# Inverse root on GpSimd, division in another slot, and spreads in column tiles: one change to a conditioned transformer block

## The chip, the cores and the metric

One core of one Trainium2 chip runs the whole kernel. The metric is the device time in microseconds (us) of one execution. TensorE multiplies matrices, VectorE and ScalarE work elementwise, GpSimd here issues DMAs that add as they write, and SyncE issues all other DMAs in its loop. The profile calls them PE, DVE, ACT, POOL and SP.

## The reference

The input x has 4 batches of 1024 tokens with 512 features; cond has 128 features for each batch. All is float32. Cut to what matters:

```python
def rmsnorm(x, t, gw, gb, bw, bb):              # t: the batch's condition
    g = (t @ gw.T + gb)[:, None, :]
    b = (t @ bw.T + bb)[:, None, :]
    return g * x * rsqrt(mean(x * x, axis=-1, keepdims=True) + 1e-6) + b

def attention(x):                                # 16 heads of 32 features
    q, k, v = heads(x @ Wq.T), heads(x @ Wk.T), heads(x @ Wv.T)
    p = softmax(einsum("blhd,bmhd->bhlm", q, k) / sqrt(32), axis=-1)
    return einsum("bhlm,bmhd->blhd", p, v).reshape(B, L, D) @ Wo.T

def swiglu(x):                                   # 2048 hidden features
    return silu(x @ gate_w.T) * (x @ hid_w.T) @ out_w.T

y = x + attention(rmsnorm(x, cond, first))
y = y + swiglu(rmsnorm(y, cond, second))
out = x + y
```

## The kernel before

**Layout.** Features lie on the 128 partitions and tokens along the free axis, in 8 blocks of 512 tokens (`NBLK`). Four heads of 32 features make a head group, and 256 queries (`HQ`) a half block. A step of the attention is one half block of queries of one head group against 256 keys. Four steps (`UN`) cover the 1024 keys, and 256 steps (`NR`) are all of the attention.

**The main loop** (line 768) runs over slots g, and each slot holds pieces of several steps: the scores of step g, the addition of the shift and the exponential of step g-5 (`r_x`), and the product with v of step g-6 (`r_v`). `kind = g % 4` is the slot's place in its round. A block has 32 slots (`BS`). The order on TensorE, VectorE, ScalarE and GpSimd is exactly the order in which the loop calls them (`manual_schedule`, line 698); what SyncE issues follows the order of the program, with a scheduler's freedom.

**Softmax.** The scores of four heads against 256 keys fill one PSUM tile (`sc`, line 310), and ScalarE copies them to `raw` (line 317). VectorE keeps an elementwise maximum in `rmax` (lines 322 and 325). In a slot of kind 0 TensorE transposes `rmax` (`mt`, line 331, full 128x128 array), VectorE reduces it to a maximum per query (line 337) and cuts minus that maximum into three bfloat16 parts, so that their sum keeps float32's accuracy (lines 339 to 342, tile `split`: 12 columns, three for each of 4 heads). In the next slot, kind 1, `parts_T` transposes the parts (`pt`, line 347), ScalarE copies the 12 rows to `mT` (line 349), and `spread` sends each head's maximum to all 128 partitions by a product with a 12x128 matrix of zeros and ones, `select` (`sp`, line 357), two heads at a time; ScalarE copies it to `shift` (line 358). `shifted` adds it to `raw` on VectorE (line 363), the exponential runs on ScalarE (line 366), and `weighted` multiplies with v (`av`, line 376).

**Row sums and division.** GpSimd's DMAs add the exponentials of steps 1, 2 and 3 of a round onto those of step 0 (line 390). In a slot of kind 0, VectorE folds the two halves (line 398), TensorE sums over partitions (line 408), ScalarE copies the sums to `total` (line 413). `inverse` takes their reciprocal (line 416, 128x256) and `normalize` multiplies with the product `avs` (line 425). Both stand at the end of that same slot of kind 0 (lines 900 to 904), ahead of the shift additions of the next slot, kind 1. For the one half block `GB`, `normalize` comes later.

**Tiling of TensorE.** `mm` (line 103) writes a product as one full-width matmul, or, if `columns[0]` is 32, as four matmuls on strips of 32 columns. Projections and feed-forward products are made of such strips in most slots; `sc` uses strips of 32 rows; `mt`, `pt` and `sp` use all columns.

**Feed-forward part.** From slot `FS` = 60 on, the slots also carry the gated feed-forward part of the block before: per two slots one chunk of 128 hidden features, with seven products in place of eight (`pair_15` to `pair_7`, tiles `pa` and `pb`) and one contraction into the output (`pc`, 32 matmuls, line 572), then the 24 chunks that are left run after the loop. Before slot 60 the slots carry the projections for keys, queries and values (`pkq`, `pv`) and the sums of weights (lines 474 to 477).

**The second norm** (lines 650 to 670; e is 32(n+1), less 4 for n > 0). For blocks n = 0 to 6: squares on ScalarE (line 132), their mean over features by a product with a constant matrix (`norm_mean`, line 145), copied to SBUF by ScalarE (line 151). All rows being alike, `compact` writes one row to DRAM (line 156), and `take` reads it back as 128x4 (`few`, line 162). At the end of slot e+20, `root` takes the square root on ScalarE (line 167), at e+20 or e+21 `invert` the reciprocal on VectorE (line 171); `put` writes the result to DRAM (line 176), and `norm_spread` reads it to all partitions (line 182). Scaling (line 193), modulation (line 196) and sums of tokens (lines 491 to 497) follow in slots g0+22 to g0+28. The norms of the first kind for later batches use a square root on ScalarE and a full reciprocal on VectorE (lines 143 and 632) in slots before 60.

What ends a slot of kind 0:

```python
            if kind == 0 and n_on and j_n < direct:
                inverse(j_n)

                if j_n != GB:
                    normalize(j_n)
            columns[0] = DH
            for fn, a in ended.pop(g, []):
                fn(*a)
```

Of the kernel before, what the change touches and what calls it, by code (L numbers as in the profile page):

```python
# [9 lines left out]

F32 = mybir.dt.float32
BF16 = mybir.dt.bfloat16
AF = mybir.ActivationFunctionType
ALU = mybir.AluOpType
# [3 lines left out]
P = 128  # L18
# [6 lines left out]
def tile_cond_transformer_block(  # L25
# [13 lines left out]
    nc = tc.nc  # L39
    NBLK, _, C, _ = x.shape  # L40
# [6 lines left out]
    DH = D // N_HEADS  # L47
    HG = P // DH
    FG = 4
    HQ = 256  # L50
# [6 lines left out]
    const = ctx.enter_context(tc.tile_pool(name="const", bufs=1))  # L57
    sb = ctx.enter_context(tc.tile_pool(name="sb", bufs=1))
# [5 lines left out]

    ident = const.tile([P, P], F32, tag="ident", name="ident")
    make_identity(nc, ident)
    ident_bf = const.tile([P, P], BF16, tag="ident_bf", name="ident_bf")
    make_identity(nc, ident_bf)
    ones_mean = const.tile([P, P], F32, tag="ones_mean", name="ones_mean")
    nc.vector.memset(ones_mean, 1.0 / D)  # L70
    ones_sum = const.tile([P, DH], F32, tag="ones_sum", name="ones_sum")
    nc.vector.memset(ones_sum, 1.0)
    eps = const.tile([P, 1], F32, tag="eps", name="eps")
    nc.vector.memset(eps, EPS)

    NP = 3 * HG
    split = [const.tile([P, QT, P], BF16, tag=f"split{i}", name=f"split{i}") for i in range(2)]
    for t in split:
        nc.vector.memset(t, 0.0)

    pick = const.tile([NP, HG], F32, tag="pick", name="pick")
    nc.vector.tensor_reduce(pick, ident[:NP, :NP].rearrange("p (h i) -> p h i", i=3), AX.X, ALU.add)
    select = const.tile([NP, HG, P], BF16, tag="select", name="select")
    nc.vector.tensor_copy(select, pick.unsqueeze(2).to_broadcast([NP, HG, P]))
    mod = const.tile([P, 4 * C, B], F32, tag="mod", name="mod")

    condT = const.tile([P, B], F32, tag="condT", name="condT")
# [15 lines left out]
    def mm(dst, w, moving, start: bool, stop: bool, seeded: bool = False):  # L103
        n = columns[0]
        for k in range(0, P, n):
            nc.tensor.matmul(  # L106
                dst[k : k + n, :], w[:, k : k + n], moving, start=start, stop=stop, skip_group_check=seeded
            )

    y, wkq, wv, wo, kq, v = {}, {}, {}, {}, {}, {}  # L110
    raw, rmax, shift, mT, av, acc, avs, oT = {}, {}, {}, {}, {}, {}, {}, {}
    x2, res, h, fw, ow = {}, {}, {}, {}, {}
    bank_a, bank_b, fifth = {}, {}, {}
    state = {}
# [13 lines left out]
    def norm_squares(dst, tag: str, k: int):  # L128

        sq = [sb.tile([P, NB], F32, tag="t", name=f"sq{tag}_{2 * k + i}", bufs=2) for i in range(2)]  # L130
        for i in range(2):
            nc.scalar.activation(sq[i], dst[:, 2 * k + i, :], AF.Square)
        if k == 0:
            state[tag] = sb.tile([P, NB], F32, tag="tot", name=f"tot{tag}", bufs=1)
            nc.vector.tensor_tensor(state[tag], sq[0], sq[1], ALU.add)
        else:
            for t in sq:
                nc.vector.tensor_tensor(state[tag], state[tag], t, ALU.add)
# [6 lines left out]
    def norm_mean(tag: str, inside: bool):  # L145
        if inside:
            pm = ps_av.tile([P, NB], F32, tag="av", name=f"pm{tag}")
        else:
            pm = ps.tile([P, NB], F32, tag="w", name=f"pm{tag}")
        mm(pm, ones_mean, state[tag], True, True)  # L150
        nc.scalar.copy(state[tag], pm)

    def compact(tag: str, t, rows: int, n: int):

# [3 lines left out]
    def take(tag: str):  # L158

        src = inv_s.pop(tag)  # L160
        few = sb.tile([P, src.shape[0] * src.shape[1] // P], F32, tag="few", name=f"few{tag}", bufs=2)
        nc.sync.dma_start(out=few, in_=src.rearrange("h (p c) -> (h p) c", c=few.shape[1]))
        state["few", tag] = few

    def root(tag: str):
        few = state["few", tag]
        nc.scalar.activation(few, few, AF.Sqrt, bias=eps)

    def invert(tag: str):
        few = state["few", tag]  # L170
        nc.vector.reciprocal(few, few)

    def put(tag: str):
        few = state.pop(("few", tag))
# [17 lines left out]
    def norm_scale(dst, tag: str, c: int):  # L192
        nc.vector.tensor_tensor(dst[:, c, :], dst[:, c, :], state[tag], ALU.mult)

    def norm_mod(which: int, b: int, dst, c: int):
        nc.scalar.activation(  # L196
            dst[:, c, :],
            dst[:, c, :],
            AF.Identity,
            bias=mod[:, (2 * which + 1) * C + c, b : b + 1],  # L200
            scale=mod[:, 2 * which * C + c, b : b + 1],
        )
# [141 lines left out]
    def parts_T(j: int):  # L344
        pt = ps.tile([P, HQ // P, P], BF16, tag="w", name=f"pt{j}")
        for qt in range(HQ // P):
            nc.tensor.transpose(pt[:, qt, :], split[j % 2][:, qt, :], ident_bf)
        mT[j] = sb.tile([NP, HQ], BF16, tag="mT", name=f"mT{j}", bufs=2)
        nc.scalar.copy(mT[j], pt[:NP, :, :].rearrange("p a b -> p (a b)"))

    def spread(j: int, k: int):

        if k == 0:
            shift[j] = sb.tile([P, HG, HQ], F32, tag="shift", name=f"shift{j}")
        pp = ps.tile([P, 2, HQ], F32, tag="w", name=f"sp{j}_{k}")
        for i in range(2):
            nc.tensor.matmul(pp[:, i, :], select[:, k + i, :], mT[j], start=True, stop=True)
        nc.scalar.copy(shift[j][:, k : k + 2, :], pp)  # L358

    def shifted(r: int, heads: slice = slice(0, HG)):  # L360
# [54 lines left out]
    def inverse(j: int):  # L415
        nc.vector.reciprocal(state["total", j], state["total", j])

    def normalize(j: int):

        m, qh = divmod(j, NB // HQ)  # L420
        n, hg = divmod(m, C)
        total = state.pop(("total", j))
        if (n, hg) not in oT:
            oT[n, hg] = sb.tile([P, NB], F32, tag=f"oT{hg}", name=f"oT{m}")
        nc.vector.tensor_tensor(oT[n, hg][:, qh * HQ : (qh + 1) * HQ], avs.pop(j), total, ALU.mult)
# [157 lines left out]
    GB = C * (NB // HQ)  # L583
    BS = GB * UN
# [9 lines left out]
    def pin(g, fn, *a):  # L594
        pinned.setdefault(g, []).append((fn, a))

    def between(g, fn, *a):
        halfway.setdefault(g, []).append((fn, a))

    def after(g, fn, *a):  # L600
        ended.setdefault(g, []).append((fn, a))
# [21 lines left out]
    for b in range(1, B):  # L623
        for half in range(QB):
            s = math.ceil((len(queue) + 1) / PACE)
            s4 = s - 4 - (s - 6) % UN
            tag = f"a{b}_{half}"
# [10 lines left out]
    FS = BS + 28  # L638
# [3 lines left out]
    for n in range(NBLK):  # L642
        g0 = (n + 1) * BS
        pin(g0 + 6, load_res, n)
        e = g0 if n == 0 else g0 - 4
        go = e + 13 if n < NBLK - 1 else g0 + 8
        for d in range(C):
            first.append((go, None, project_out, (n, d)))
            pin(go - 3 + (d // 2 * 4 if n else 0), load_wo, n, d)
        if n < NBLK - 1:  # L650
            tag = f"f{n}"
            after(e + 16, add_res, n)
            for k in range(2):
                after(e + 15 + k, lambda n=n, tag=tag, k=k: norm_squares(x2[n], tag, k))
            if n == 0:
                between(e + 17, norm_mean, tag, False)
            else:
                amid.setdefault(e + 17, []).append((norm_mean, (tag, True)))
            after(e + 17, norm_compact, tag)
            after(e + 19, take, tag)  # L660
            after(e + 20, root, tag)
            after(e + (20 if n == 0 else 21), invert, tag)
            after(e + (21 if n == 0 else 22), put, tag)
            after(e + (22 if n == 0 else 24), norm_spread, tag)
            scales, mods = ((24, 24, 25, 25), (25, 25, 26, 26)) if n == 0 else ((22, 22, 24, 24), (23, 23, 25, 25))
            for c in range(C):
                after(g0 + scales[c], lambda n=n, tag=tag, c=c: norm_scale(x2[n], tag, c))
                between(g0 + mods[c], lambda n=n, c=c: norm_mod(1, n // QB, x2[n], c))
            for i in range(4):
                after(g0 + (26, 26, 27, 28)[i] - (n > 0 and i == 0), token_sums, n, i)  # L670
# [27 lines left out]
    with tc.manual_schedule(  # L698
# [35 lines left out]
        direct = NR // UN - 2  # L734
        late = None
        g = 0
# [31 lines left out]
        while g < END:  # L768
            kind = g % UN
# [6 lines left out]
            j_n = g // UN - 3  # L776
            n_on = 0 <= j_n < NR // UN
            ffn = g >= FS
            p = (g - FS) // 2
# [3 lines left out]
            if kind == 1 and m_on:  # L783
                parts_T(j_m)
# [77 lines left out]
            else:  # L862
# [34 lines left out]
                    chain(g)()  # L897
                for fn, a in halfway.pop(g, []):
                    fn(*a)
            if kind == 0 and n_on and j_n < direct:  # L900
                inverse(j_n)

                if j_n != GB:
                    normalize(j_n)
            columns[0] = DH
            for fn, a in ended.pop(g, []):
                fn(*a)
# [4 lines left out]
        n = NBLK - 1  # L912
# [6 lines left out]
        for p in range(p0, NP_):  # L919
# [25 lines left out]
            if p == p0:  # L945
                pm = ps.tile([P, NB], F32, tag="w", name=f"pmf{n}")
# [54 lines left out]
```

## Time and profile before

| | |
|---|---|
| median of 3 runs | 2452.37 us (2448.12 to 2452.83) |
| the profiled execution | 2447.08 us, its span 2445.3 us, granted TensorE clock 0.997 |
| ScalarE's table loads, 1283 ns each | 13 before the exponential (L366), 7 at L167, 5 at L143, 4 elsewhere |
| VectorE's reciprocal of `total` (L416) | 64 of 1744 ns |
| VectorE's product with `avs` (L425) | 64 of 425 ns |
| spreads (L357), 12x128 weights, bfloat16 | 256 matmuls, 270 ns each |
| transposes of the parts (L347) | 128 matmuls, 219 ns each |
| ScalarE's square root of 128x4 (L167), VectorE's reciprocal of it (L171) | 7 of 298 ns, 7 of 169 ns |

A line of the timeline gives the start in us, the length, the engine, the line of the kernel, the operation, the written and the read tile, and how many instructions follow each other; in brackets the idle time ahead of it, and what ended it. Matmuls overlap, so a matmul's length is its latency, and the distance between the starts of two groups is what the first one takes of TensorE's time. A line of the waits gives who waited for whom, the total in us, how often, and the longest.

### The profile page before, as it was taken

The numbers are of one execution on the slowest core, as the hardware profiler recorded it, in microseconds if no ns is written. First come the engines' busy times: TensorE is split into PE (matmuls) and PEld (weight loads), VectorE is DVE, ScalarE is ACT, GpSimd is POOL, SyncE is SP. The second block draws the span as 40 slices with busy tenths as digits, with TensorE's granted clock in tenths as the row PEclk, the third lists the DMA queues.
The fourth block names the chain that finished last, engine by engine and source line by source line (L and its number), as shares of the span: only waits on it lengthen the run. The fifth ranks groups of instructions, "written<-read, shape, count | busy, mean of one in ns | idle before, by whom it ended". The sixth has DMA issues, their size and how long they took to land. (4 is left out here: it accounts for less than half of the span.)

```text
span 2445.3 us, 71149 instructions
## 1 busy us (share of the span) xinstructions
PE 2386.7 (98%) x31785; PEld 1128.7 (46%) x31785; DVE 1938.9 (79%) x2180; ACT 1416.2 (58%) x1495; POOL 172.8 (7%) x207
## 2 busy tenths in 40 slices
PE   8999999999999999999999999999999999999999
PEld 3333333334445544545454544454455445444544
DVE  2688888878889988999799979997999889843332
ACT  3677777666566655666566656665666566512110
POOL 0000000000000000000000000000000000000000
PEclk9999999999999999999999999999999999999999
DMA  6599999988888988889788988888888888853442
GB/s 214 168 284 253 250 256 235 232 205 216 206 201 208 220 224 197 208 215 234 195 208 208 237 206 197 209 226 211 206 205 206 226 200 205 212 165 118 143 129 71
DMA packets 185983, 501.70 MB, mean 205 GB/s; under 512 B 21319, under 2 KB 78663, under 8 KB 158286
## 3 DMA queue, kind: packets, MB, share of 16 engines
q0 software_dynamic: 28656, 208.68, 44.2%
q1 hardware_dynamic: 156734, 288.47, 35.5%
q8 instruction: 250, 4.10, 0.7%
q14 instruction: 55, 0.45, 0.1%
q10 hardware_dynamic: 288, 0.01, 0.0%
HBM read 246.44 MB, written 41.97 MB: 118 GB/s over the span
## 5 line engine op out<-in xcount | busy, mean ns | idle before, releaser
L317 ACT COPY raw<-sc 128x2048 f32<-128x2048 f32 x256 | 479.4, 1873 | 200.1 <-PE sc L310 133.4
L363 DVE TENSOR_TENSOR raw<-raw,shift 128x2048 f32<-128x2048 f32 (+1 forms) x320 | 589.0, 1856 | 3.3 <-ACT shift L358 2.8
L366 ACT ACTIVATE raw<-raw 128x2048 f32<-128x2048 f32 x256 | 490.2, 1915 | 128.9 <-DVE raw L363 124.8
L322 DVE TENSOR_TENSOR rmax<-rmax,raw 128x1024 f32<-128x1024 f32 x384 | 469.5, 1223 | 54.4 <-ACT raw L317 47.9
L106 PE MATMUL pc<-h,ow 128*32 128x512 f32 x4096 | 467.7, 593 | 3.3 <-DMA ow<-in_out_w 2.3
L376 PE MATMUL av<-raw,v 128*32 128x256 f32 x4096 | 275.8, 387 | 34.5 <-ACT raw L366 30.6
L390 POOL DMA_DIRECT2D raw<-raw x192 | 165.7, 863 | 1959.3 <-ACT raw L366 886.0
L310 PE MATMUL sc<-q,k 32*128 32x256 f32 x4096 | 293.3, 400 | 0.3 <-ACT raw L317 0.3
L106 PE MATMUL pa<-x,fa 128*32 128x256 f32 x4096 | 268.2, 379 | 0.3 <-DVE pa L524 0.2
L106 PE MATMUL pa<-sums,fw 128*32 128x256 f32 x4096 | 267.9, 379 | 0.0
L106 PEld LDWEIGHTS pc<-h,ow 128*32 128x32 f32 x4096 | 128.2, 110 | 246.7 <-issue 225.4
L310 PEld LDWEIGHTS sc<-q,k 32*128 32x128 f32 x4096 | 184.9, 184 | 116.6 <-issue 66.6
L106 PE MATMUL pkq<-y,wkq 128*32 128x512 f32 (+1 forms) x1664 | 234.3, 601 | 4.2 <-ACT y L196 4.1
L376 PEld LDWEIGHTS av<-raw,v 128*32 128x32 f32 x4096 | 107.4, 109 | 159.0 <-ACT raw L366 52.2
L106 PEld LDWEIGHTS pa<-x,fa 128*32 128x32 f32 x4096 | 131.1, 110 | 103.0 <-issue 8.8
L106 PEld LDWEIGHTS pa<-sums,fw 128*32 128x32 f32 x4096 | 133.1, 110 | 87.9
L577 DVE SCALAR_TENSOR_TENSOR res<-pc,res 128x512 f32<-128x512 f32 x128 | 88.2, 689 | 76.0 <-PE pc L106 75.0
L556 ACT ACTIVATE t<-pa 128x512 f32<-128x512 f32 x128 | 77.5, 605 | 109.9 <-PE pa L106 109.5
L539 ACT COPY pb<-pa 128x256 f32<-128x256 f32 x128 | 45.9, 359 | 160.3 <-PE pa L106 158.9
L106 PE MATMUL pb<-x,fw 128*32 128x256 f32 x2048 | 134.0, 379 | 1.2 <-ACT pb L539 1.2
L106 PE MATMUL pa<-x,fw 128*32 128x256 f32 x2048 | 135.2, 381 | 0.0
L106 PEld LDWEIGHTS pkq<-y,wkq 128*32 128x32 f32 (+1 forms) x1664 | 73.2, 118 | 131.5 <-issue 118.3
(106 smaller groups left out, 2214.4 us busy)
## 6 DMA issues: line engine op xcount, KB each, us to landing
raw<-raw POOLq DMA_DIRECT2D x192, 1024.0 KB, 9.1
fw<-sw SPq DMA_DIRECT2D x128, 512.0 KB, 7.5
fa<-in_gh_w SPq DMA_DIRECT2D x128, 384.0 KB, 6.5
ow<-in_out_w SPq DMA_DIRECT2D x128, 256.0 KB, 3.7
wkq<-in_kq_w SPq DMA_DIRECT2D x32, 512.0 KB, 5.9
v<-vs SPq DMA_DIRECT2D x128, 128.0 KB, 5.5
k<-kqs SPq DMA_DIRECT2D x124, 128.0 KB, 6.8
kqs<-st SPq DMA_DIRECT2D x61, 256.0 KB, 7.4
```

The source lines that it names most:

```text
L106: nc.tensor.matmul(dst[k : k + n, :], w[:, k : k + n], moving, start=start, stop=stop, skip_group_check=seeded)
L310: nc.tensor.matmul(sc[:, i, k, :], keys[rows, k * P : (k + 1) * P], queries[rows, :], start=True, stop=True)
L317: nc.scalar.copy(raw[r].rearrange("p k h q -> p h k q"), state.pop(("sc", r)))
L322: nc.vector.tensor_tensor(rmax[j], rmax[j], raw[r][:, k, :, :], ALU.max)
L363: nc.vector.tensor_tensor(t, t, s.unsqueeze(1).to_broadcast(list(t.shape)), ALU.add)
L366: nc.scalar.activation(raw[r], raw[r], AF.Exp)
L376: nc.tensor.matmul(av[j][i * DH : (i + 1) * DH, :], v[m, u][:, k, i * DH : (i + 1) * DH], raw[r][:, k, i, :], start=(kt == 0), stop=(kt == ...
L390: nc.gpsimd.dma_start(out=acc[j].rearrange("p k h q -> p (k h q)"), in_=raw[r].rearrange("p k h q -> p (k h q)"), accum_op=ALU.add,)
L539: nc.scalar.copy(bank_b[p][:, RIGHT], bank_a[p][:, RIGHT])
L556: nc.scalar.activation(state["t", p], bank_a[p], AF.Tanh, scale=0.5)
L577: nc.vector.scalar_tensor_tensor(r, pp, 0.5, r, ALU.mult, ALU.add)
```

## The change

It has four parts.

1. *Inverse root.* `norm_mean` now adds epsilon as it copies (Identity with a bias, for Copy). `root` and `invert` are replaced by `inverse_root`, all at the end of slot e+20: one VectorE instruction shifts the number's bits right by one and inverts them against a constant, which gives a first estimate of the inverse root up to a factor; GpSimd multiplies by that factor and takes four Newton steps of four instructions, 17 instructions on 128x4, each waiting for the one before. `put` stays where it was and reads GpSimd's result. In the built program these 17 stand in the Pool queue between the accumulate DMAs of slots e+20 and e+21, and SyncE's `put` keeps its place, between the `ow` load and the spread.
2. *Division.* `inverse` and `normalize` move from the end of a slot of kind 0 to the end of the slot two later (kind 2, the third), for all slots of kind 0 before 60 but that of the last half block of a token block, and from 60 on for those at places 12, 24 and 28 of a block. All others stay.
3. *Spreads.* `select` and `mT` get 128 rows, zero below the 12, and `spread` goes through `mm`: eight matmuls on strips of 32 columns for two on all columns. `mT` is two fixed tiles.
4. *Transposes of the parts* take 32 columns of `split` for 128.

```diff
--- before.py
+++ after.py
@@ -9,6 +9,7 @@
 from concourse._compat import with_exitstack
 
 F32 = mybir.dt.float32
+I32 = mybir.dt.int32
 BF16 = mybir.dt.bfloat16
 AF = mybir.ActivationFunctionType
 ALU = mybir.AluOpType
@@ -80,8 +81,14 @@
 
     pick = const.tile([NP, HG], F32, tag="pick", name="pick")
     nc.vector.tensor_reduce(pick, ident[:NP, :NP].rearrange("p (h i) -> p h i", i=3), AX.X, ALU.add)
-    select = const.tile([NP, HG, P], BF16, tag="select", name="select")
-    nc.vector.tensor_copy(select, pick.unsqueeze(2).to_broadcast([NP, HG, P]))
+
+
+    select = const.tile([P, HG, P], BF16, tag="select", name="select")
+    nc.vector.memset(select, 0.0)
+    nc.vector.tensor_copy(select[:NP], pick.unsqueeze(2).to_broadcast([NP, HG, P]))
+    parts_of = [const.tile([P, HQ], BF16, tag=f"mT{i}", name=f"mT{i}") for i in range(2)]
+    for t in parts_of:
+        nc.vector.memset(t, 0.0)
     mod = const.tile([P, 4 * C, B], F32, tag="mod", name="mod")
 
     condT = const.tile([P, B], F32, tag="condT", name="condT")
@@ -148,7 +155,7 @@
         else:
             pm = ps.tile([P, NB], F32, tag="w", name=f"pm{tag}")
         mm(pm, ones_mean, state[tag], True, True)
-        nc.scalar.copy(state[tag], pm)
+        nc.scalar.activation(state[tag], pm, AF.Identity, bias=eps)
 
     def compact(tag: str, t, rows: int, n: int):
 
@@ -158,17 +165,24 @@
     def take(tag: str):
 
         src = inv_s.pop(tag)
-        few = sb.tile([P, src.shape[0] * src.shape[1] // P], F32, tag="few", name=f"few{tag}", bufs=2)
+        few = sb.tile([P, src.shape[0] * src.shape[1] // P], F32, tag="few", name=f"few{tag}")
         nc.sync.dma_start(out=few, in_=src.rearrange("h (p c) -> (h p) c", c=few.shape[1]))
         state["few", tag] = few
 
-    def root(tag: str):
+    def inverse_root(tag: str):
+
         few = state["few", tag]
-        nc.scalar.activation(few, few, AF.Sqrt, bias=eps)
-
-    def invert(tag: str):
-        few = state["few", tag]
-        nc.vector.reciprocal(few, few)
+        y, t = (sb.tile(list(few.shape), F32, tag=f"few{i}", name=f"few{i}{tag}") for i in range(2))
+        nc.vector.tensor_scalar(
+            y.bitcast(I32), few.bitcast(I32), 1, 0x3FFFFFFF, ALU.logical_shift_right, ALU.bitwise_xor
+        )
+        nc.gpsimd.tensor_scalar_mul(y, y, 1.35 * 2.0**62)
+        for _ in range(4):
+            nc.gpsimd.tensor_tensor(t, y, y, ALU.mult)
+            nc.gpsimd.tensor_tensor(t, t, few, ALU.mult)
+            nc.gpsimd.tensor_scalar(t, t, -0.5, 1.5, ALU.mult, ALU.add)
+            nc.gpsimd.tensor_tensor(y, y, t, ALU.mult)
+        state["few", tag] = y
 
     def put(tag: str):
         few = state.pop(("few", tag))
@@ -344,9 +358,9 @@
     def parts_T(j: int):
         pt = ps.tile([P, HQ // P, P], BF16, tag="w", name=f"pt{j}")
         for qt in range(HQ // P):
-            nc.tensor.transpose(pt[:, qt, :], split[j % 2][:, qt, :], ident_bf)
-        mT[j] = sb.tile([NP, HQ], BF16, tag="mT", name=f"mT{j}", bufs=2)
-        nc.scalar.copy(mT[j], pt[:NP, :, :].rearrange("p a b -> p (a b)"))
+            nc.tensor.transpose(pt[:DH, qt, :], split[j % 2][:, qt, :DH], ident_bf)
+        mT[j] = parts_of[j % 2]
+        nc.scalar.copy(mT[j][:NP], pt[:NP, :, :].rearrange("p a b -> p (a b)"))
 
     def spread(j: int, k: int):
 
@@ -354,7 +368,7 @@
             shift[j] = sb.tile([P, HG, HQ], F32, tag="shift", name=f"shift{j}")
         pp = ps.tile([P, 2, HQ], F32, tag="w", name=f"sp{j}_{k}")
         for i in range(2):
-            nc.tensor.matmul(pp[:, i, :], select[:, k + i, :], mT[j], start=True, stop=True)
+            mm(pp[:, i, :], select[:, k + i, :], mT[j], True, True)
         nc.scalar.copy(shift[j][:, k : k + 2, :], pp)
 
     def shifted(r: int, heads: slice = slice(0, HG)):
@@ -658,8 +672,7 @@
                 amid.setdefault(e + 17, []).append((norm_mean, (tag, True)))
             after(e + 17, norm_compact, tag)
             after(e + 19, take, tag)
-            after(e + 20, root, tag)
-            after(e + (20 if n == 0 else 21), invert, tag)
+            after(e + 20, inverse_root, tag)
             after(e + (21 if n == 0 else 22), put, tag)
             after(e + (22 if n == 0 else 24), norm_spread, tag)
             scales, mods = ((24, 24, 25, 25), (25, 25, 26, 26)) if n == 0 else ((22, 22, 24, 24), (23, 23, 25, 25))
@@ -897,11 +910,16 @@
                     chain(g)()
                 for fn, a in halfway.pop(g, []):
                     fn(*a)
-            if kind == 0 and n_on and j_n < direct:
-                inverse(j_n)
-
-                if j_n != GB:
-                    normalize(j_n)
+            if n_on and j_n < direct and kind in (0, 2):
+
+
+                at = g - kind
+                in_first = j_n % GB == GB - 1 or (at >= FS and at % BS not in (12, 24, 28))
+                if in_first == (kind == 0):
+                    inverse(j_n)
+
+                    if j_n != GB:
+                        normalize(j_n)
             columns[0] = DH
             for fn, a in ended.pop(g, []):
                 fn(*a)
```

## The prediction

> **What bounds the kernel now.** I read the page first, then the waits of TensorE, then the timeline engine by engine. In what follows a slot is one pass of the main loop, a round is four slots (kind 0 to 3), about 31 us once the feed-forward part runs beside the attention, and a block is 32 slots, 256 us.
>
> ```profile
> span 2445.3 us, 71149 instructions
> PE 2386.7 (98%) x31785; PEld 1128.7 (46%) x31785; DVE 1938.9 (79%) x2180; ACT 1416.2 (58%) x1495; POOL 172.8 (7%) x207
> ...
> DVE  2688888878889988999799979997999889843332
> ```
>
> TensorE is the bound: 98% busy, and the same groups of matmuls follow at the same pitch over the whole run. What can be won is therefore (a) pitch, where the tiling of the array changes, and (b) the few places where TensorE waits. VectorE is at 8 to 9 tenths in the same slices, so it is the next bound.
>
> ```profile
> PE av L376 <- ACT raw L366: 30.6, 24, 3.5
> ...
> PE av L376 <- ACT totf L151: 3.3, 6, 0.6
> PE sum L408 <- PE pa L106: 2.8, 7, 0.7
> ```
>
> Nearly all waiting is `av` waiting for the exponential, 24 times. The next view is TensorE's timeline, first a slot with spreads (`sp`), then one without:
>
> ```profile
> 1197.41 1.05 PE L106 MATMUL pb<-x,fw 128*32 128x256 f32 x16
> 1198.40 0.27 PE L347 MATMUL pt<-ident_bf,split 128*128 128x128 bf16 x2
> 1198.60 1.15 PE L310 MATMUL sc<-q,k 32*128 32x256 f32 x16
> 1199.57 0.38 PE L357 MATMUL sp<-mT,select 12*128 12x256 bf16 x2
> 1199.88 1.07 PE L376 MATMUL av<-raw,v 128*32 128x256 f32 x16
> 1200.88 0.39 PE L357 MATMUL sp<-mT,select 12*128 12x256 bf16 x2
> 1201.20 1.07 PE L106 MATMUL pa<-x,fw 128*32 128x256 f32 x16
> ...
> 1213.60 1.05 PE L106 MATMUL pb<-x,fw 128*32 128x256 f32 x16
> 1214.57 1.15 PE L310 MATMUL sc<-q,k 32*128 32x256 f32 x16
> 1215.65 1.07 PE L376 MATMUL av<-raw,v 128*32 128x256 f32 x16
> ```
>
> Differences of starts are the true pitch: pb to sc 0.97, sc to av 1.08, av to pa 0.89, and pa to pa, with no change of tiling, 0.86. Last, three engines at two of the waits:
>
> ```profile
> 1235.37 1.28 ACT L366 ACT_TABLE_LOAD   x1
> 1236.66 1.91 ACT L366 ACTIVATE raw<-raw 128x2048 f32<-128x2048 f32 x1
> 1238.62 1.07 PE L376 MATMUL av<-raw,v 128*32 128x256 f32 x16 [1.27 <-ACT raw L366]
> ...
> 1307.69 2.29 DVE L363 TENSOR_TENSOR raw<-raw,shift 128x2048 f32<-128x2048 f32 x1
> ...
> 1315.62 0.64 PE L408 MATMUL sum<-raw,ones_sum 128*32 128x256 f32 x8 [0.36 <-PE pa L106]
> ```
>
> In the first three a table load delays the exponential and av stands 1.27. In the last two VectorE runs without a gap from 1301.6 to 1317.6, and the sum waits for the fold (L398) at its end.
>
> **What the Trainium skill says.** "TensorEngine Tiling (Array Packing)", Key Properties: a change of tiling mode drains TensorE. The trace agrees: 0.97 against 0.86 after pb. "ScalarE activation tables: per-element evaluation and per-set limits" puts two sets one load of 1283 ns apart; the trace has just that. "SBUF — State Buffer", Who interferes with whom: a VectorE instruction with two SBUF inputs and a GpSimd instruction that reads SBUF block each other fully. No run here shows it yet: GpSimd issues only DMAs after the start. "GPSIMD Engine Reference", section 3.1, prices long elementwise work alone, not 4 elements.
>
> **The change, part by part.** Signs: minus is time saved.
>
> *Spreads and part transposes on 32-column tiles.* The shown slot takes 0.99+0.20+0.97+0.31+1.00+0.32 = 3.79 from pb to pa. Then: pb to pt without a change of tiling 0.86 (-0.13); pt to sc, two transposes in one strip plus the 0.11 of a change, 0.22 to 0.29, I take 0.26 (+0.06); sc to sp like sc to av (+0.11); the first spread, now eight matmuls, unknown: at best two groups of four at the 0.10 that a full-width one now takes (0.20), at worst the fp32 rate of 0.054 each (0.43), I take 0.24 (-0.07); av to sp 0.89 (-0.11). Sum up to the second spread -0.14, bounds -0.22 and +0.08. Behind it ScalarE leads: shift copy, raw copy, avs copy and exponential follow without a gap, and end 0.12 before av is due in an ordinary round (1268.23 against 1268.35); a waiting av follows by 0.06. So of the 0.08 won on the second spread only 0.03 to 0.06 counts (-0.03; at worst +0.15, as a slower spread delays that chain). -0.17 over 50 rounds with feed-forward is -8.5 (-14 to +11). In the 13 early rounds the chain before pt is full-width, so that a change of tiling is added: zero.
>
> *Root and reciprocal to VectorE bits and GpSimd.* Seven square roots with their table loads go; the load that delays the exponential costs TensorE 1.28 each time (waits of 1.27 six times, 1.29 at 493.47), ScalarE being free at 1235.37: 7 x 1.28 = -9.0. Added are one VectorE instruction of about 0.18 (row L339), in a slot where the shift addition ends about 0.3 before ScalarE is free, and 17 GpSimd instructions in series. None of that kind is in the trace: at least 0.10 each (the memset at the start), at most the length of the VectorE instruction that each waits for, 1.22 to 2.28. I take 0.3, so 5 us, done near 1238, before `put` is issued now (1240.96). Behind them in the Pool queue stands one accumulate DMA (now 1231.78, landing in 9.1, its fold at 1252.6): 11 us spare. VectorE held up in turn: +1 over all (0 to +3). The copy with the epsilon bias is 0.10 longer (0.69 of L143 against 0.59); the exponential ahead of it comes 0.9 earlier: zero. Zeroing of the new tiles lies in VectorE's idle start.
>
> *Division to the third slot, before the feed-forward part.* There reciprocal and product (1.74 and 0.42, 2.1 from start to start) stand before the shift addition of the second slot. The waits of av there are 3.46, 1.99, 0.26, 2.00, 3.46, 1.48 and 1.13 (at 160, 227, 260, 294, 361, 427, 461); each falls by at most 2.1: 11.1. Evictions queued behind those exponentials hold banks: two av groups of 1.94 for 1.07, and 64 matmuls in 8.74 for 7.54: 2.9. In the round of 227 the division lands behind four scalings and delays the next exponential by 0.7. Together -13.3. Elsewhere VectorE has gaps of 1.5 to 2.7 in the third and fourth slots.
>
> *The same in the feed-forward part, three rounds of each block.* At the third slot VectorE has no gap up to the fold. Round 24, in full: without the division the exponential starts at 1296.16, behind the avs copy, for 1296.86, so av's wait of 0.68 goes and all is 0.67 earlier. Then 2.08 is put ahead of the addition at 1307.69, which starts 1.41 later; its exponential ends at 1313.35, av was due at 1311.79, so it waits 1.6; fold ends at 1316.95, sum was due at 1316.0 and starts at 1317.05 for 1315.62: +1.4 net. Round 12: 0.62 saved at 1207.55, then 0.34 before av and 0.4 before the sum: +0.1. Round 28: 0.1 saved; then the fold has 1.07 and the exponential 1.13 of spare, against 1.9: +0.8. A check in the present trace: two scalings (1.29) in this very place of the round before leave 0.59 and 0.12 of those spares. 2.3 over six blocks, and 0.8 once at slot 60: +14.6. Bounds: -9 if only the present waits go, +17.
>
> Sum: -8.5 - 9.0 + 1.0 - 13.3 + 14.6 = -15.2. The profiled execution took 2447.1 with a span of 2445.3; that gives 2431.9. The median of the runs, 2452.4, is 5.3 above the profiled one; I carry the difference over: 2437.
>
> **Rivals.** *The moved divisions cost nothing in the feed-forward part*: the three waits of 0.62, 0.74 and 0.13 just vanish, -9 for +14.6, 2413. For it: the three rounds chosen are those with the waits. Against: no gap on VectorE. *Column-tiled spreads are bound by issue* at 0.054: +0.23 per round for -0.17, so 20 more, 2457. For it: no bf16 matmul on 32 columns is in the trace. Against: the four fp32 matmuls of a group start 6 ns apart. *The GpSimd chain comes too late* (slower): `put` stands in SP's queue ahead of the spread DMAs and the next `ow` (issued 1244.91, landing in 3.7, needed at 1256.4). It decides from 15 us, 0.9 per instruction. If each one waits for a VectorE instruction of 1.3, the chain ends near 1254.7, `ow` lands near 1262.4, and pc stands 5.9 in six blocks: 2437+35 = 2472. For it: VectorE runs two-input additions and maxima most of the time. Against: the gate's instructions and evictions read PSUM and leave the port free. That the change does not do what it says: the sets could still switch; but the Identity of L196 causes no load now.
>
> **How the numbers follow.** Forecast 0.53 (own range 2427 to 2447), moved divisions free 0.17, issue-bound spreads 0.14, late GpSimd chain 0.09, and 0.07 for a smaller gain between. 0.2% is about what a measurement of this kernel can tell from no change: under 2447.5 is faster, over 2457.3 slower. Faster: 0.50+0.17+0.02+0.07 = 0.76; same: 0.03+0.09 = 0.12; slower: 0.09+0.03 = 0.12. The range 2412 to 2456 leaves out the late chain, half of the issue-bound case and the lower edge of the free one.
>
> **What would show it.** Right: no table load at L167 or behind it; sp to av near 0.24 and av to sp 0.89; no av wait over 1.5 before 600; new waits at slots 26 to 28 of each block, sum and av together 2 to 3. Wrong: sp to av over 0.35; no wait there; GpSimd ending after 15 us, or pc waiting for `ow`.

## The result, and the profile after

The change makes the kernel slower: 2482.65 us median of 4 runs (2479.17 to 2488.46), against 2452.26 (2448.12 to 2452.83) before, a ratio of 1.0131 (95% interval 1.0116 to 1.0145); the ratio is that of all runs, and the two medians alone give 1.0124. The prediction, 2437, and its whole range, 2412 to 2456, lie below that. The profiled execution took 2479.17, its span is 2477.4, the granted TensorE clock 0.991 for 0.997.

First the lines of the page after, then the longest waits of TensorE (who waited for whom, us in total, times, longest).

```profile
span 2477.4 us, 72785 instructions
...
PE 2393.6 (97%) x32553; PEld 1138.5 (46%) x32553; DVE 1940.5 (78%) x2183; ACT 1392.2 (56%) x1474; POOL 248.9 (10%) x326
...
DVE  2688888888789978898889978997899798843332
...
POOL 0000000200020002000110002000200020000000
```

```profile
PE sum L422 <- DVE raw L412: 28.0, 6, 5.0
PE av L390 <- ACT raw L380: 25.2, 30, 1.6
...
PE pa L113 <- DVE pa L538: 3.9, 20, 0.2
PE pc L113 <- DMA ow<-in_out_w: 2.4, 1, 2.4
PE sum L422 <- PE pa L113: 2.2, 5, 0.4
```

VectorE and ScalarE are no busier than before. New is the first wait: six times, once behind the second norm of each of blocks 1 to 6, the sum of the exponentials waits for VectorE's fold (L412), 28.0 us in all; before, the view has no wait of that name, only seven short ones of the sum, up to 0.7, that it puts down to `pa`; the prediction read one of them as a wait for the fold. The waits of `av` for the exponential have become shorter (longest 1.6 for 3.5) and more (30 for 24). `pc` waits for `ow` once, as before. The line of GpSimd shows the seven chains, six times as a 2 and once spread over two slices.

One of the six waits, followed back through three engines. TensorE (start, length; in brackets the idle time and what ended it):

```profile
1253.41 1.05 PE L113 MATMUL pa<-sums,fw 128*32 128x256 f32 x16
1258.97 0.95 PE L422 MATMUL sum<-raw,ones_sum 128*32 128x256 f32 x8 [4.51 <-DVE raw L412]
1259.85 1.97 PE L345 MATMUL mt<-ident,rmax 128*128 128x128 f32 x8
1261.75 4.03 PE L113 MATMUL pc<-h,ow 128*32 128x512 f32 x32
1265.60 1.04 PE L113 MATMUL pb<-x,fw 128*32 128x256 f32 x16
```

VectorE, which the sum waited for:

```profile
1233.39 2.35 DVE L377 TENSOR_TENSOR raw<-raw,shift 128x1024 f32<-128x1024 f32 x2
1235.94 2.49 DVE L336 TENSOR_TENSOR rmax<-rmax,raw 128x1024 f32<-128x1024 f32 x2 [0.19 <-ACT raw L331]
1238.34 0.43 DVE L538 TENSOR_TENSOR pa<-pa,p 128x256 f32<-128x256 f32 x1
...
1240.18 2.28 DVE L377 TENSOR_TENSOR raw<-raw,shift 128x2048 f32<-128x2048 f32 x1
...
1257.64 1.23 DVE L412 TENSOR_TENSOR raw<-raw 128x1024 f32<-128x1024 f32 x1 [5.58 <-DMA raw<-raw]
```

And GpSimd, which issues the DMA that the fold waited for:

```profile
1233.58 1.12 POOL L179 TENSOR_SCALAR few0f<-few0f 128x4 f32<-128x4 f32 x1 [8.88 <-DVE few0f L176]
1234.78 1.02 POOL L181 TENSOR_TENSOR few1f<-few0f 128x4 f32<-128x4 f32 x1
1235.88 0.20 POOL L182 TENSOR_TENSOR few1f<-few1f,fewf 128x4 f32<-128x4 f32 x1
1236.16 1.05 POOL L183 TENSOR_SCALAR few1f<-few1f 128x4 f32<-128x4 f32 x1
1237.30 1.18 POOL L184 TENSOR_TENSOR few0f<-few0f,few1f 128x4 f32<-128x4 f32 x1
1238.56 0.20 POOL L181 TENSOR_TENSOR few1f<-few0f 128x4 f32<-128x4 f32 x1
...
1240.24 2.27 POOL L183 TENSOR_SCALAR few1f<-few1f 128x4 f32<-128x4 f32 x1
...
1245.55 0.20 POOL L184 TENSOR_TENSOR few0f<-few0f,few1f 128x4 f32<-128x4 f32 x1
1246.03 1.81 POOL L404 DMA_DIRECT2D raw<-raw  x2 [0.28 <-issue]
```

Read from below. The accumulate DMA of the round's last step leaves at 1246.03, and the one after it, which is not late, right behind it (x2). It stood in GpSimd's queue behind the 17 instructions of the chain, which takes 12.2 us (1233.58 to 1245.75). The fold starts when that DMA has landed, 11.6 after its issue. The 17 fall into two kinds: ten take 0.20, and seven take 1.0 to 2.3. Each long one lies beside a VectorE instruction with two inputs in SBUF and ends within 0.1 of it: the 2.27 from 1240.24 ends at 1242.51, the addition from 1240.18 at 1242.46. While VectorE reads PSUM (`pa`, 1238.34, and the two behind it), the instructions of the chain go through at 0.20.

### The profile page after: what moved, and what is told of

Its sections match the earlier page's. It is cut to its first block, busy times and chain, and to the rows that moved or that the text cites. A ratio compares the mean times of both kernels' runs of the same rounds, so it can differ in the third digit from the quotient of the medians.

```text
span 2477.4 us, 72785 instructions
## 1 busy us (share of the span) xinstructions
PE 2393.6 (97%) x32553; PEld 1138.5 (46%) x32553; DVE 1940.5 (78%) x2183; ACT 1392.2 (56%) x1474; POOL 248.9 (10%) x326
## 5 line engine op out<-in xcount | busy, mean ns | idle before, releaser
L336 DVE TENSOR_TENSOR rmax<-rmax,raw 128x1024 f32<-128x1024 f32 x384 | 469.5, 1223 | 47.4 <-ACT raw L331 41.7
L113 PEld LDWEIGHTS pa<-x,fa 128*32 128x32 f32 x4096 | 124.2, 110 | 119.2 <-DVE pa L538 22.5
L113 PE MATMUL pb<-sums,fa 128*32 128x256 f32 x2048 | 134.0, 379 | 0.0
```

The source lines that it names most:

```text
L113: nc.tensor.matmul(dst[k : k + n, :], w[:, k : k + n], moving, start=start, stop=stop, skip_group_check=seeded)
L336: nc.vector.tensor_tensor(rmax[j], rmax[j], raw[r][:, k, :, :], ALU.max)
```

## The experiments

Eight kernels, each against the kernel before on the same chip. Theory when they were made: *queue*, the accumulate DMA behind the chain is the whole loss. Rivals: *late put*, what costs is that the inverse root itself is ready late; and for the gains, the prediction's own terms.

**The chain behind the DMA.** The 17 instructions in the middle of slot e+21, after that slot's accumulate DMA; the estimate by shift stays where it was (block 0 unchanged).

```diff
-            after(e + 20, inverse_root, tag)
+            if n == 0:
+                after(e + 20, inverse_root, tag)
+            else:
+                after(e + 20, estimate, tag)
+                amid.setdefault(e + 21, []).append((newton, (tag,)))
```

> The changed kernel, with one thing moved: for the blocks 1 to 6 the 17 GpSimd instructions are called in the middle of slot e+21, behind that slot's accumulate DMA in the Pool queue, and no longer ahead of it. The estimate on VectorE, the number of instructions, put and all else stay. Queue theory (the chain holds up the third accumulate DMA of the round, the fold waits for it, and TensorE cools down meanwhile): the six waits of the sum of 4.3 to 5.2 us go, and with them the slower mt and pc behind them, together about 41 us, so 2441 us. Rival, late put (the loads that pile up on SP behind put crowd the DMA engines, and that is what makes the accumulate land late): put is as late as before, so at least 3 of each 5 us stay, 2462 us or more.

Measured: 2438.15, ratio 0.9960 (0.9945 to 0.9974), span 2433.8, 43.6 under that of the change. GpSimd's and VectorE's timelines at the same place:

```profile
1218.61 0.86 POOL L425 DMA_DIRECT2D raw<-raw  x1 [8.11 <-DMA raw<-raw]
1219.55 0.95 POOL L200 TENSOR_SCALAR few0f<-few0f 128x4 f32<-128x4 f32 x1
...
1231.36 0.20 POOL L205 TENSOR_TENSOR few0f<-few0f,few1f 128x4 f32<-128x4 f32 x1
1231.87 0.90 POOL L425 DMA_DIRECT2D raw<-raw  x1 [0.31 <-issue]
```

```profile
1219.20 2.35 DVE L398 TENSOR_TENSOR raw<-raw,shift 128x1024 f32<-128x1024 f32 x2
...
1237.78 1.22 DVE L433 TENSOR_TENSOR raw<-raw 128x1024 f32<-128x1024 f32 x1
```

The chain is as long (12.0) and ends at the same point of the loop: 12.4 after the start of VectorE's addition (1219.20), for 12.4 after 1233.39 in the changed kernel. Only its place against the DMA differs, the fold waits for nothing, and no sum waits for a fold any more. That excludes the late `put` as a cause by itself: the inverse root is no earlier here, and `put` leaves 12.4 after the addition in both kernels. How long the two accumulate DMAs of this fence took from issue to landing (KB each, then us), first the one ahead of the chain, then the one behind it, which goes out together with `put` and the loads after it:

```profile
raw<-raw POOLq DMA_DIRECT2D x1, 1024.0 KB, 8.6
...
raw<-raw POOLq DMA_DIRECT2D x1, 1024.0 KB, 11.8
```

**The old root in the changed kernel.** ScalarE's square root and VectorE's reciprocal back, the other parts as changed.

```diff
...
-            after(e + 20, inverse_root, tag)
+            after(e + 20, root, tag)
+            after(e + (20 if n == 0 else 21), invert, tag)
```

> The changed kernel with the old root: square root on ScalarE, reciprocal on VectorE, copy without epsilon; moved divisions, column-tile spreads and narrow transposes stay. Queue theory and late put alike: minus 41 us of waits and slow matmuls, plus 9 us of table loads, 2450 us, and no wait of the sum over 1.5 us. Rival, that the moved divisions or the spreads make the long waits: 2475 us or more.

Measured: 2449.5, ratio 1.0003 (0.9994 to 1.0012). So the other three parts together bring nothing that can be measured, where the prediction's terms make -7.2, and no sum waits for a fold. Against the run above (same chip) the old root costs 11.4: without the delay of the DMA the new root is a gain.

**The new root alone**, in the kernel before.

```diff
...
-            after(e + 20, root, tag)
-            after(e + (20 if n == 0 else 21), invert, tag)
+            after(e + 20, inverse_root, tag)
```

> The kernel before with the inverse root on GpSimd alone; divisions, spreads and transposes as before. Queue theory and late put alike: 2452 minus 9 of table loads plus 41, about 2484 us, with six waits of the sum of about 5 us. If the waits need the moved divisions too: 2443 to 2455 us.

Measured: 2481.54, ratio 1.0132 (1.0113 to 1.0151). This part alone makes the whole loss. The sum waits for the fold 29.1 here, in eight waits of 1.0 to 6.4.

**The feed-forward divisions back in the first slot**, in the changed kernel.

```diff
-                in_first = j_n % GB == GB - 1 or (at >= FS and at % BS not in (12, 24, 28))
+                in_first = j_n % GB == GB - 1 or at >= FS
```

> The changed kernel, with all divisions from slot 60 on back in the first slot of the round; those before slot 60 stay moved. By the prediction's count (0.1, 1.4 and 0.8 for three rounds of each of six blocks, and 0.8 once) this saves 14.6 us: 2468 us. By the rival, that the moved divisions are free there, it costs 9 us: 2492 us.

Measured: 2469.32, ratio 1.0086 (1.0064 to 1.0107), 0.0045 or 11 us under the changed kernel (5 to 17, from the intervals of the two ratios).

**Both mends together:** the chain behind the DMA, and those divisions in the first slot.

```diff
-            after(e + 20, inverse_root, tag)
...
+                after(e + 20, estimate, tag)
+                amid.setdefault(e + 21, []).append((newton, (tag,)))
...
-                in_first = j_n % GB == GB - 1 or (at >= FS and at % BS not in (12, 24, 28))
+                in_first = j_n % GB == GB - 1 or at >= FS
```

> The two mends together: the 17 GpSimd instructions behind the accumulate of slot e+21, and all divisions from slot 60 on back in the first slot. The first mend took 44.5 us off the changed kernel, the second 13.3. If they are independent, 2438 minus 13 to 14: 2424.5 us, 1% under the kernel before. If VectorE or GpSimd merely shifts the wait elsewhere: no less than 2435 us.

Measured: 2425.55, ratio 0.9905 (0.9887 to 0.9923), span 2420.9. It beats both kernels. Its waits of TensorE:

```profile
PE av L411 <- ACT raw L401: 17.5, 24, 1.6
```

With the divisions moved (first experiment) that line is 25.4 in 30 waits, and 21 waits of `pa` for VectorE, 4.1 in all, come on top, of which 2 with 0.3 are left here. In return six waits of `av` for ScalarE's copy to `totf`, 4.4 in all, are back, as before the change. The step from the first experiment to this one is 0.0055, 13.5 us (8 to 19). These waits make 7 of it; most of the rest is busy time of TensorE, 2372.5 for 2378.4, whose cause was not traced.

**The spreads and the transposes of the parts alone**, in the kernel before.

```diff
...
-            nc.tensor.transpose(pt[:, qt, :], split[j % 2][:, qt, :], ident_bf)
+            nc.tensor.transpose(pt[:DH, qt, :], split[j % 2][:, qt, :DH], ident_bf)
...
-            nc.tensor.matmul(pp[:, i, :], select[:, k + i, :], mT[j], start=True, stop=True)
+            mm(pp[:, i, :], select[:, k + i, :], mT[j], True, True)
```

> The kernel before with the column-tile spreads and narrow transposes alone. From the pitches in the trace of the changed kernel, 3.64 us for 3.79 in a round from pb to pa, less 0.05 that av then waits for the exponential, 0.11 is won in each of 50 rounds and about as much in 13 early ones: minus 6 to 7, a ratio of 0.9975. By the prediction (0.17 for 50 rounds): minus 8.5, 0.9965. If ScalarE's chain behind the second spread takes back all: 0.999 or more.

Measured: 2447.11, ratio 0.9991 (0.9983 to 1.0000): 2.2 us, between 0 and 4. The gain is smaller than the prediction's count and than the one made from the trace after; the expectation that ScalarE's chain takes back all of it is nearest, and not excluded. The wait of `av`:

```profile
PE av L383 <- ACT raw L373: 36.4, 32, 3.7
```

Before it was 30.6 in 24 waits. TensorE's distances in a round with spreads are 0.16 shorter (below), 8 us over 50 rounds, and 5.8 of them are found again in this one line. Where TensorE already waited for ScalarE, arriving sooner only lengthens the wait: six waits of 1.27 or 1.28 behind a table load have become 1.39.

**The early divisions alone**, in the kernel before.

```diff
...
+                in_first = j_n % GB == GB - 1 or at >= FS
+                if in_first == (kind == 0):
+                    inverse(j_n)
...
```

> The kernel before with the divisions before slot 60 moved to the third slot, and nothing else. The prediction's count is minus 13.3, a ratio of 0.9946. The waits that stand in the changed kernel's trace before 560 us (three rounds with a new wait of 0.66 to 0.86 in the slot behind the moved division, two that keep 1.64) say minus 9 to 10, 0.996. If moving only shifts the wait: 0.999 or more.

Measured: 2442.87, ratio 0.9961 (0.9944 to 0.9978), 9.6 us; the prediction's 0.9946 is in the interval, the count from the trace after (0.996) is nearer. What stays and what is new, on TensorE:

```profile
158.25 1.07 PE L379 MATMUL av<-raw,v 128*32 128x256 f32 x16 [1.34 <-ACT raw L369]
205.41 1.07 PE L379 MATMUL av<-raw,v 128*32 128x256 f32 x16 [0.55 <-ACT raw L369]
237.31 1.07 PE L379 MATMUL av<-raw,v 128*32 128x256 f32 x16 [0.61 <-ACT raw L369]
```

The wait of 3.46 falls to 1.34, as predicted (by 2.1), and waits of 0.5 to 0.6 arise in four rounds (205, 237, 301, 334), where one of 0.7 was predicted, with one of 1.29 at 431.

**A chain half as long in the bad place.** Two of the four Newton steps are left out, so that the inverse root is rougher; 9 instructions for 17, still ahead of the DMA.

```diff
-        for _ in range(4):
+        for _ in range(2):
```

> The changed kernel with two of Newton's four steps left out (the inverse root is rougher), so 9 GpSimd instructions for 17, still ahead of the accumulate DMA. In the trace of the changed kernel the ninth ends 6.0 us after the first begins, the seventeenth 12.2 after. If what counts is the chain's length against the slack of the third accumulate (about 9 us), the waits of the sum of 4.3 to 5.2 us go entirely: 2438 to 2443 us. If any work ahead of the accumulate delays the fold in proportion: waits of 2 to 2.5 us stay, 2460 us.

Measured: 2437.90, ratio 0.9950 (0.9932 to 0.9968). GpSimd:

```profile
1221.55 1.12 POOL L179 TENSOR_SCALAR few0f<-few0f 128x4 f32<-128x4 f32 x1 [8.87 <-DVE few0f L176]
...
1227.37 0.20 POOL L184 TENSOR_TENSOR few0f<-few0f,few1f 128x4 f32<-128x4 f32 x1
1227.85 0.90 POOL L404 DMA_DIRECT2D raw<-raw  x1 [0.28 <-issue]
```

The DMA leaves 6.3 after the start of the chain, for 12.45 with four steps, and the loss is gone: none of the six waits of 4 to 5 is left. (The one wait for a fold, 1.5 at 2157.58, is that of the last round; the spreads alone and the early divisions alone, both with the old root, have it too, with 1.4 and 1.6.) Half the chain doesn't cost half; the cost begins somewhere between the two lengths.

## Why the prediction was wrong, step by step

**The step that failed: "17 GpSimd instructions in series [...] I take 0.3, so 5 us".** The chain took 12.2. With that the "11 us spare" behind it, a term that was itself right, was spent, and a term put at nothing became a loss of 42.

*The chain: 5 us predicted, 12.2 measured.* The bounds in the prediction held the truth: 0.10, and the length of a VectorE instruction, 1.22 to 2.28. The value between was a guess. The trace gives 0.20 plus 0.08 to the next one for a free instruction, and 1.0 to 2.3 for a blocked one: 8.9 for seven, 2.0 for ten, 1.3 in between. The prediction named the right part of the Trainium skill ("SBUF — State Buffer", Who interferes with whom: a VectorE instruction with two SBUF inputs and a GpSimd instruction that reads SBUF block each other), and the trace now agrees for GpSimd's side, the only one that was held up here; but it was weighed by a feeling for how often the port is free. It could have been worked out: between 1233.39 and 1244.86 VectorE spends 9.6 us in additions and maxima with two SBUF inputs (2.35, 2.49, 2.28, 2.48), and a chain gets on only in the gaps: six instructions go through in the one of 1.84 us at 1238.34.

*The spare: 11 us predicted, 10.6 measured.* In the first experiment the DMA lands at 1227.2 (1218.61 and 8.6), and VectorE comes to the fold at 1237.78. In the changed kernel the DMA would have left near 1232.8 (1218.61, moved by the 14.19 between the two starts of VectorE's addition). It left 13.2 later, and it landed in 11.6 for 8.6, another 3.0. These 16.2, less the 10.6, are the fold's wait of 5.58; at the old landing time it would have been 2.6, an estimate from the same figures. The prediction counted with one landing time, 9.1, wherever the DMA stood. The half chain puts the DMA off by 7.1, it lands in 10.3, and the spare holds.

Why a late DMA lands more slowly is not shown. It leaves 0.25 behind `put` (1245.78), among the loads that follow `put`, and right ahead of the next accumulate. The second accumulate isn't needed for it: in the first experiment a single one among those loads takes 11.8, and in one round of the new root alone the fold starts 8.3 after the first of two that leave together (1259.47 to 1267.73), and the sum waits only 1.1. In that round the loads go out later, the read of the norm 3.8 behind `put` for 1.4 in the changed kernel. That points to `put`'s loads. So the late `put` costs nothing by itself, but it may have made the waits longer.

*The price of a wait was more than its length.* 28.0 of waiting explains only two thirds of the 43.6 between the changed kernel and the first experiment. The rest is time in which TensorE counts as busy, 2393.6 for 2378.4. Most of it is a slower clock after each wait. The 8 us behind the wait in the changed kernel, and the same slot in the first experiment (columns: busy time and instructions of TensorE, weight loads, VectorE, ScalarE, GpSimd; then the granted clock, DMA share, GB/s):

```profile
1258.97:1266.97 8.00, 8.00 (x70) 3.49 (x74) 6.03 (x9) 3.24 (x5) 0.85 (x1) 0.79 1.05 339
```

```profile
1240.09:1248.09 8.00, 8.00 (x106) 3.87 (x102) 6.65 (x10) 3.20 (x5) 0.86 (x1) 1.00 1.05 344
```

At a clock of 0.79, 8 us lose 1.7. The timeline agrees: sum to `mt` 0.88 for 0.54, `mt` to `pc` 1.90 for 1.02, `pc` to `pb` 3.85 for 3.46, together 1.6 more. Behind the six waits the clock is 0.68, 0.79, 0.79, 0.66, 0.75 and 0.79, which makes 12.3; with the 28.0 that is 40 of the 43.6. The Trainium skill, "TensorE: Matmul & The Clock Gate", Part 1, says that the array is throttled after an idle window of about 3.4 us and released by activity; the six waits, 4.1 to 5.0 long, agree. Shorter ones can have it too: behind two of the six waits of 1.57 in the blocks' rounds 24 (1318.86 and 2110.75) the clock is 0.79 as well, from 1 to 9 us after them. The forecast had no such term.

**The slower rival** had the right mechanism, a GpSimd chain that ends late, and took 1.3 for each instruction, 22 us in all, where 0.72 and 12.2 were measured. It named the wrong victim: `put`, then `ow`, deciding from 15 us. `put` did leave late, 12.4 after VectorE's addition for 8.5 before (1240.96, the addition at 1232.46), and the first experiment shows that this by itself costs nothing. The DMA in GpSimd's own queue decided, at a chain shorter than those 15. The prediction named that DMA, then gave its spare to a chain of 5 and didn't test the spare at its own upper bound, nor in this rival.

**The other steps.**

| step | predicted, us | measured, us | from |
|---|---|---|---|
| spreads and transposes | -8.5 | -2.2 (-4 to 0) | alone |
| table loads, less VectorE held up | -8.0 | -11.4 (-15 to -6) | new root in the right place against the old one |
| early divisions | -13.3 | -9.6 (-13.7 to -5.4) | alone |
| divisions in the feed-forward part | +14.6 | +11 (5 to 17) and +13.5 (8 to 19) | put back, twice |
| the chain ahead of the DMA | 0 | +42 (37 to 47) | changed kernel against the first experiment, 0.0171 |

The ranges come from the 95% intervals of the ratios. The sum, with 12 for the fourth, is +31; measured are 0.0131 x 2452 = +32. The first three alone predict -23 for the kernel with both mends, and 0.0095 x 2449 = -23 came out.

*Spreads.* A slot of the changed kernel with spreads:

```profile
1198.18 1.05 PE L113 MATMUL pb<-x,fw 128*32 128x256 f32 x16
1199.17 0.27 PE L361 MATMUL pt<-ident_bf,split 128*32 128x128 bf16 x2
1199.38 1.15 PE L324 MATMUL sc<-q,k 32*128 32x256 f32 x16
1200.45 0.40 PE L113 MATMUL sp<-mT,select 128*32 128x256 bf16 x8
1200.68 1.04 PE L390 MATMUL av<-raw,v 128*32 128x256 f32 x16
1201.55 0.40 PE L113 MATMUL sp<-mT,select 128*32 128x256 bf16 x8
1201.76 1.04 PE L113 MATMUL pa<-x,fw 128*32 128x256 f32 x16
```

sp to av is 0.23 (0.24 predicted, a guess between 0.20 and 0.43 that hit), sc to sp 1.07 (+0.11, as predicted), av to sp 0.87 here and 0.92 in the median. But pb to pt stays at 0.99: the transposes still pay for a change although they now take 32 columns, so the 0.13 there doesn't come; pt to sc stays 0.2, which spares the predicted 0.06. "Issue-bound spreads" is excluded. The median round is 3.63 from pb to pa for 3.79, -0.16; from there to the next av it is 4.72 for 4.66, so -0.10 stays. -0.10 x 50 would be -5; the rest went into the longer waits of the sixth experiment. The prediction asked of the second spread whether ScalarE takes the gain back, and not of the slots in which TensorE already waited.

*Table loads.* Right; that the gain is larger than counted lies within the noise. The table loads at the square root (7 before) are gone, and those ahead of the exponential fall from 13 to 6. In the waits the gain is seen as well: against the changed kernel with the old root, the first experiment has 25.4 for 35.5 us of `av`'s waits, 30 for 37 of them, 1.44 each for the 1.28 that was counted.

*Early divisions.* Right in kind. The groups of 1.94 that the prediction put down to held banks are better read as a slow clock: the trace of before shows a clock of 0.86 between 156 and 168, around the wait of 3.46, and with the division moved it is 1.00 in the same stretch.

*Divisions in the feed-forward part.* Right in place, and in size as far as the two ranges tell. The wait of 1.6 behind the moved division of round 24 is there, with a short one that was not foreseen:

```profile
1055.93 1.07 PE L390 MATMUL av<-raw,v 128*32 128x256 f32 x16 [1.57 <-ACT raw L380]
1057.20 1.07 PE L113 MATMUL pa<-x,fa 128*32 128x256 f32 x16 [0.20 <-DVE pa L538]
```

The rival "moved divisions free" is excluded by the two kernels that put them back: both became faster.

## What to carry to other kernels

Before small serial work is put on an engine that "only issues DMAs", write down what stands behind it in that queue and by when it has to land, and test that spare at the upper bound of the work's cost, not at a guess in the middle. For GpSimd in this kernel that bound comes from VectorE's timeline: beside VectorE's instructions with two SBUF inputs the chain got on by one instruction for each of them. Test also whether the transfer lands as fast at the later time; here it took 11.6 for 8.6. In this kernel one place further back in the queue, behind the DMA and not ahead of it, made 42 us of difference and turned the loss into a gain.

## What was not expected of the hardware

- A GpSimd instruction on 128x4 took 0.20 us with VectorE on PSUM operands, and up to 2.27 beside a VectorE addition in SBUF; VectorE's own were not longer for it (none of the 384 maxima at L336 took over 1227 ns, as at L322 before).
- A wait of TensorE of 4 to 5 us cost another 1.7 to 2.7 in slow matmuls, with a granted clock of 0.66 to 0.79 in the 8 us behind it.
- An accumulate DMA of 1 MB landed 8.6 us after its issue in its usual place, and 11.2 to 12.1 after it in the six rounds in which it left together with `put`, its loads and the next accumulate.
- Two transposes into 32 columns left pb to pt at 0.99, the same as into 128 columns, where two products on 32 columns follow each other in 0.86.
